# One graph-attention layer on one core: constants behind the first k|v tiles, three empty steps in a tile's tail, a third PSUM tile for projections

## The chip, the cores and the metric

The kernel runs on one core of a Trainium2 chip, in one launch. The metric is the device time of one execution in microseconds (us). Engines are called by the profile's names: PE (matmuls), PEld (loading of its weights), DVE (vector), ACT (scalar, activations), POOL (GpSimd, which also issues the indirect DMAs) and SP (which only issues DMAs).

## The reference

There are 4096 nodes with rows of 512 floats, 8 heads of 64, and an adjacency matrix of 4096 x 4096 with about 0.4% ones besides the diagonal. Everything is float32.

```python
hs = layer_norm(x, ln1_scale, ln1_bias)          # sources
ht = layer_norm(h_target, ln1_scale, ln1_bias)   # targets
q = (ht @ Wq + bq).reshape(T, H, HD) / sqrt(HD)
k = (hs @ Wk + bk).reshape(S, H, HD)
v = (hs @ Wv + bv).reshape(S, H, HD)
logits = where(adj != 0, einsum('thd,shd->hts', q, k), -1e30)
ctx = einsum('hts,shd->thd', softmax(logits), v).reshape(T, D)
ht = ht + (ctx @ Wo + bo)
ht = layer_norm(ht, ln2_scale, ln2_bias)
ff = gelu(ht @ W1) @ W2                           # 512 -> 2048 -> 512
out = plain_norm(x + ht + ff)                     # mean and variance only
```

All node masks are one. If a row had too many edges for the kernel's lists, or another of its assumptions failed, a flag set by `verdict` would send the launch through a second, dense path; with these inputs it does not run.

## The kernel before, in words

The kernel uses the sparsity: per target only the rows of k and v at its edges are fetched. Work comes in tiles of 128 rows.

**Lists.** `edges(i)` reads the 128 adjacency rows of tile i in four quarters of 512 KB (tile "a", two buffers, issued by SP), ACT turns them into signs ("sg", L670), DVE multiplies them with column numbers (L672) and picks the largest in segments (L674), and a few more DVE steps make the list of the row's neighbours. `sort(part)` orders the targets of a part (20 tiles in part A, 12 in part B) by their number of edges; POOL scatters the records into that order by indirect DMAs (L783). A tile of sorted targets then needs only as many slots as its richest row has edges; these numbers are fixed in the tables `CAPS_A` and `CAPS_B` (11 to 40).

**Projections.** `project` walks over groups of two tiles. `norm` loads the rows ("xin", three buffers), DVE takes the statistics, POOL the power -1/2 (L643), and ACT scales. `turn` transposes the group on PE (L834) and ACT copies it out of PSUM into "hT" (L838). For a source tile, `source` makes k and v in two halves of eight matmuls each (L848) into the PSUM tile "pq", ACT copies each half to "row" (L850), and ACT's queue stores the row to the DRAM table kvd (L852). For a target tile, `target` makes q into "pq" (L859); DVE scales it into "row" with the bias bq8 (L862), DVE or POOL fill the other half of "row" with the normed target row times s1b plus bob (L867, L868), and the row goes to the table tqd (L870). "pq" has two buffers, "row" has two. The order is six x groups, then x and h groups by turns, then the remaining h groups.

**Constants.** `late_constants` loads Wq, Wo and four broadcast rows (s1b, b1b, bob, bq8) on SP's queue, zeroes the first row of kvd, scales bq (L619), and makes bv @ Wo on PE into a "pq" tile (L623), which DVE adds to bob (L625, L626). b1b sits in a "row" buffer until L625 has read it. It is called right after the first norm and transposes, ahead of all projections.

**Attention.** A sorted tile is handled in kv segments of up to three slots (210 in all). `issue` lets POOL gather the kv rows of a segment (L895, six kv buffers, four segments ahead) and, at a tile's first segment, the target rows "tq" (three buffers). Per segment DVE multiplies k by q (L1054) and sums per head (L1058), ACT takes the exponential (L1062, L1072), DVE and ACT multiply v (L1019, L1039), and PE adds up the transposed products in "cps" (L1027). When a tile's last segment is through, its tail `finish` runs: sums, 1/sum, copied wide by ACT (L959); transposes of that on PE (L964); copy (L966); multiplication with cps on DVE (L968); product with Wo on PE (L972); sum with the target row on DVE (L975), which is the last reader of "tq"; and for the last tile of a group of two, shift, power, scaling (L987), transposes (L995) and the copy into h2T (L999). `finish` is a generator. At each yield it hands control back, and `attention` calls `advance` twice per segment, each call moving every living tail by one step. The single PSUM buffer "t" serves all tail products.

**Feed-forward.** `feed(g)` waits for h2T of group g, then makes 512 -> 2048 (L1152), gelu on ACT (L1155), and 2048 -> 512 (L1161); `end` adds x, norms and scatters the rows to the output.

**Order.** `_weave` runs several generators in the order of their written costs: a stream that yields a cost is moved on by it, and the stream with the smallest time is served next. In the first weave the streams are `projections`, `prepare` (lists of part A, sort, first prefetch), `fill` and `begin` (first attention steps); in the second one `attention`, the feeds and the lists of part B. What this gives is the order of the program and so the priority of its instructions; the framework places them on the engines' queues, each of which then runs in order.

`projections`, the stream that the change alters, is short:

```python
def projections():
    yield from _some(proj, both * G)
    src.close()
    load_quarter(late.enter_context(tc.tile_pool(name="s2wa", bufs=1)), 0)
    yield from proj
```

`_some(proj, n)` passes on n costs of `proj`, one per k|v or q tile. G is 2, so 2 * G is four tiles.

Of the kernel before, what the change touches and what calls it, by code (L numbers as in the profile page):

```python
# [8 lines left out]
F32 = mybir.dt.float32  # L9
# [8 lines left out]
P = 128  # L18
# [413 lines left out]
def _some(gen, n):  # L432

    while n:
        cost = next(gen, StopIteration)
        if cost is StopIteration:
            return
        n -= cost is not None
        yield cost
# [3 lines left out]
def adj_resnorm_kernel(  # L443
# [34 lines left out]
    N, D = x.shape  # L478
# [4 lines left out]
    G = 2  # L483
# [46 lines left out]
    with tc.tile_pool(name="keep", bufs=1) as keep:  # L530
# [14 lines left out]
        with ExitStack() as late:  # L545
# [61 lines left out]
            def late_constants():  # L607
                zero = wp.tile([P, 2 * D // P], F32, name="zero")
                nc.vector.memset(zero, 0.0)
                nc.sync.dma_start(kvd[0:1, :].rearrange("o (p n) -> (o p) n", p=P), zero)  # L610
                wq = load_w(wp, Wq, "wq", nc.sync)
                nc.sync.dma_start(wo, Wo.rearrange("(c p) n -> p c n", p=P))
                s1b = row_bcast(wp, ln1_scale, "s1b")
                b1b = ip.tile([P, 2 * D], F32, name="row")[:, :D]
                nc.sync.dma_start(b1b, bass.AP(tensor=ln1_bias.tensor, offset=ln1_bias.offset,
                                               ap=[[0, P], [1, D]]))
                bob = row_bcast(wp, bo, "bob")
                bq8 = row_bcast(wp, bq, "bq8")
                nc.vector.tensor_scalar_mul(bq8, bq8, HD ** -0.5)  # L619

                pb = psi.tile([P, D], F32, name="pq", bufs=2)
                for kc in range(KC):
                    nc.tensor.matmul(pb, bvc[:, kc:kc + 1].to_broadcast([P, P]), wo[:, kc, :],  # L623
                                     start=kc == 0, stop=kc == KC - 1)
                nc.vector.tensor_add(bob, bob, b1b)  # L625
                nc.vector.tensor_add(bob, pb, bob)  # L626
                return wq, s1b, bob, bq8
# [166 lines left out]
            def project(order, t=None):  # L794


                state = {}

                def scaled(t, rs, nm):
                    nc.scalar.activation(t, t, AF.Identity, bias=nm, scale=rs)  # L800

                def norm(n, t=None):
                    if n >= len(order):
                        return
                    kind, g = order[n]
                    if t is None:
                        t = ip.tile([P, G, D], F32, name="xin", bufs=3)
                        nc.sync.dma_start(t, rows(x if kind == "x" else h_target, g))
                    if kind == "h" and g * G >= NA:
                        rs, nm = hnorm[0]  # L810
                        for j in range(G):
                            i = g * G + j - NA
                            scaled(t[:, j, :], rs[:, i:i + 1], nm[:, i:i + 1])
                        state[n] = t
                        return
                    mv = ip.tile([P, G, 2], F32, name="mv")
                    for j in range(G):
                        stats(ip, t[:, j, :], mv[:, j, :], "n1")
                    rs, nm = rstd_of(ip, mv, G, "n1")
                    for j in range(G):  # L820
                        scaled(t[:, j, :], rs[:, j:j + 1], nm[:, j:j + 1])
                    state[n] = t

                def turn(n):
                    if n >= len(order):
                        return
                    t = state[n]
                    hT = ip.tile([P, KC, GR], F32, name="hT")
                    for k2 in range(KC // 2):
                        pt = (psi if k2 else ps).tile([P, 2, GR], F32, name="pt" if k2 else "t")  # L830
                        for k in range(2):
                            kc = k2 * 2 + k
                            for j in range(G):
                                nc.tensor.transpose(pt[:, k, j * P:(j + 1) * P],  # L834
                                                    t[:, j, kc * P:(kc + 1) * P], ident)
                        for k in range(2):
                            kc = k2 * 2 + k
                            nc.scalar.activation(hT[:, kc, :], pt[:, k, :], AF.Identity,  # L838
                                                 bias=b1c[:, kc:kc + 1], scale=s1c[:, kc:kc + 1])
                    state[n] = t, hT  # L840

                def source(n, j):
                    g, hT = order[n][1], state[n][1]
                    kvr = ip.tile([P, 2 * D], F32, name="row")
                    for half, w in enumerate((wk, wv)):
                        pkv = psi.tile([P, D], F32, name="pq", bufs=2)
                        for kc in range(KC):
                            nc.tensor.matmul(pkv, hT[:, kc, j * P:(j + 1) * P], w[:, kc, :],  # L848
                                             start=kc == 0, stop=kc == KC - 1)
                        nc.scalar.copy(kvr[:, half * D:(half + 1) * D], pkv)  # L850
                    r0 = 1 + (g * G + j) * P
                    nc.scalar.dma_start(kvd[r0:r0 + P, :], kvr)  # L852
                    return 7.8

                def target(n, j):
                    g, (t, hT) = order[n][1], state[n]
                    pq = psi.tile([P, D], F32, name="pq", bufs=2)
                    for kc in range(KC):
                        nc.tensor.matmul(pq, hT[:, kc, j * P:(j + 1) * P], wq[:, kc, :],  # L859
                                         start=kc == 0, stop=kc == KC - 1)  # L860
                    tq = ip.tile([P, 2 * D], F32, name="row")
                    nc.vector.scalar_tensor_tensor(tq[:, :D], pq, HD ** -0.5, bq8,  # L862
                                                   op0=ALU.mult, op1=ALU.add)
                    part = 1 if g * G >= PARTS[1][0] else 0

                    eng, dma = (nc.vector, nc.sync) if ready else (nc.gpsimd, nc.gpsimd)
                    eng.tensor_mul(tq[:, D:], t[:, j, :], s1b)  # L867
                    eng.tensor_add(tq[:, D:], tq[:, D:], bob)  # L868
                    r0 = (g * G + j - PARTS[part][0]) * P
                    dma.dma_start(tqd[part][r0:r0 + P, :], tq)  # L870
                    return 4.3

                with tc.manual_schedule(engines={mybir.EngineType.DVE}):
                    norm(0, t)
                    turn(0)
                    norm(1)
                yield 0.0
                for n, (kind, _) in enumerate(order):
                    while n + 2 < len(order) and order[n + 2][0] == "h" \
                            and order[n + 2][1] * G >= NA and not hnorm:  # L880
                        yield None
                    for j in range(G):
                        cost = (source if kind == "x" else target)(n, j)
                        if j == 0:
                            turn(n + 1)
                        else:
                            norm(n + 2)
                            del state[n]
                        yield cost
# [53 lines left out]
            def finish(i, p, cps, group, hs, mv):  # L943
# [15 lines left out]
                nc.scalar.copy(rxf.rearrange("p (h d) -> p h d", h=H),  # L959
                               ri.unsqueeze(2).to_broadcast([P, H, HD]))  # L960
                yield
                prx = ps.tile([P, KC, P], F32, name="t")
                for c in range(KC):
                    nc.tensor.transpose(prx[:, c, :], rxf[:, c * P:(c + 1) * P], ident)  # L964
# [1 line left out]
                nc.scalar.copy(ct, prx)  # L966
                yield
                nc.vector.tensor_mul(ct, cps, ct)  # L968
                yield
                pa = ps.tile([P, D], F32, name="t")  # L970
                for c in range(KC):
# [13 lines left out]
                nm = negmean(sp, mv[:, :nh, :], rs, nh, "n2")  # L985
                for j, h in enumerate(hs):
                    nc.scalar.activation(h, h, AF.Identity, bias=nm[:, j:j + 1], scale=rs[:, j:j + 1])  # L987
                yield
                w = len(hs) * P
                h2T = sp.tile([P, KC, 2 * P], F32, name="h2T")  # L990
# [229 lines left out]
            proj = project(order, first_x)  # L1220
            next(proj)
            list_constants()
            wq, s1b, bob, bq8 = late_constants()
            w1, w2 = [], []

            def load_quarter(pool, q):
# [3 lines left out]
                nc.sync.dma_start(w2[q], W2[q * D:(q + 1) * D, :].rearrange("(c p) n -> p c n", p=P))  # L1230

            def projections():
                yield from _some(proj, both * G)
                src.close()
                load_quarter(late.enter_context(tc.tile_pool(name="s2wa", bufs=1)), 0)
                yield from proj
# [86 lines left out]
```

## Time and profile before

| | us |
|---|---|
| median of 5 runs | 1905.1 |
| lowest, highest | 1896.77, 1911.73 |
| profiled execution | 1909.35 |
| its span on the core | 1907.3 |

The profile's page lists the busy time of each engine (matmul ends are modelled, so a busy PE need not be PE at its peak), the span in 40 slices with the granted PE clock and the DMA share, the chain of work that ended last, and the costliest groups of instructions. The largest groups are these.

| line | engine, what | count | busy us |
|---|---|---|---|
| L895 | POOL, issue of the kv gathers | 600 | 701.8 |
| L1161 | PE, 2048 -> 512 | 1024 | 470.8 |
| L1152 | PE, 512 -> 2048 | 2176 | 473.5 |
| L1054 | DVE, k by q | 210 | 351.5 |
| L1058 | DVE, sum per head | 210 | 349.6 |
| L1027 | PE, transposes of v products | 2092 | 268.6 |
| L1019 | DVE, v by weights | 210 | 249.1 |
| L848 | PE, k and v products | 512 | 122.7 + 119.5 |

A wait is idle time of an engine in front of an instruction, put down to what released that instruction. The releaser is inferred, and of several the last is named.

### The profile page before, as it was taken

Reading aid. Unit: us, or ns where it says so; the run is one execution under the profiler, and the core shown is the slowest. Engines: PE = TensorE matmul, PEld = TensorE weight load, DVE = VectorE, ACT = ScalarE, POOL = GpSimd, SP = SyncE. Lnnn points to the kernel's source line nnn. Section 1 sums busy time; section 2 is a strip of 40 time slices with the busy share of each in tenths; the row PEclk is TensorE's granted clock in tenths of the full one; section 3 lists DMA queues with packets and bytes.
Section 4 is the critical chain, followed back from the end, with each engine's and each line's share of the span. In section 5 each row is a group of like instructions: output and inputs, shape, how many; then the busy total and the mean of one; then the engine's idle time right before and its main releaser. Section 6 shows DMA issues by size and latency. Waiting matters only on the chain.

```text
span 1907.3 us, 22630 instructions
## 1 busy us (share of the span) xinstructions
PE 1707.1 (90%) x6974; PEld 1090.4 (57%) x6974; DVE 1506.5 (79%) x2712; ACT 1180.9 (62%) x2943; POOL 938.5 (49%) x847
## 2 busy tenths in 40 slices
PE   6799888687789989988999998988998999999995
PEld 2344343344557666655767675766665766667664
DVE  4778887556989999876787888889999999989601
ACT  4666655444658777565666757676776777766510
POOL 1003322423555445466666665767766777666201
PEclk9999999898999999999999999999998999999998
DMA  8888886689979787666777877889888788777200
GB/s 290 273 273 294 278 260 225 199 315 385 344 272 318 270 319 242 217 223 223 240 256 250 287 265 264 308 276 306 299 280 298 247 300 295 235 266 273 95 1 24
DMA packets 155738, 490.48 MB, mean 257 GB/s; under 512 B 24900, under 2 KB 29592, under 8 KB 155608
## 3 DMA queue, kind: packets, MB, share of 16 engines
q0 software_dynamic: 99040, 355.28, 53.9%
q1 hardware_dynamic: 50864, 114.78, 18.2%
q10 hardware_dynamic: 5704, 18.89, 2.6%
q8 instruction: 57, 0.93, 0.2%
q14 instruction: 73, 0.60, 0.1%
HBM read 441.23 MB, written 47.65 MB: 256 GB/s over the span
## 4 chain that ended last, share of the span: by engine, by line
DVE 25%; DMA 25%; PE 23%; issue 10%; POOL 9%; ACT 6%; SPq 0%; DVEq 0%; POOLq 0%; ACTq 0%
DMA kv<-kvd,rec 12%; DMA a<-in_adj_dram 8%; PE pf L1152 7%; DVE kv L1054 7%; PE po L1161 7%; POOL kv L895 6%; DVE lg L1058 6%; DVE kv L1019 4%; PE t L972 3%; PE cps L1027 3%; ACT sg L670 2%; POOL rec L783 1%; ACT kv L1039 1%; DVE n_st L653 1%; DMA xin<-in_x_dram 1%
## 5 line engine op out<-in xcount | busy, mean ns | idle before, releaser
L895 POOL DMA_INDIRECT kv<-kvd,rec x600 | 701.8, 1170 | 406.2 <-issue 181.2
L1161 PE MATMUL po<-w,gt 128*128 128x512 f32 x1024 | 470.8, 600 | 8.5 <-ACT gt L1155 8.5
L1152 PE MATMUL pf<-h2T,w 128*128 128x256 f32 (+1 forms) x2176 | 473.5, 370 | 1.9 <-ACT h2T L999 1.8
L1054 DVE TENSOR_TENSOR kv<-kv,tq 128x1536 f32<-128x1536 f32 (+2 forms) x210 | 351.5, 1676 | 136.0 <-DMA kv<-kvd,rec 125.8
L1152 PEld LDWEIGHTS pf<-h2T,w 128*128 128x128 f32 x2176 | 388.5, 192 | 67.9 <-issue 20.6
L1039 ACT ACTIVATE kv<-kv,pa 128x64 f32<-128x64 f32 x1512 | 389.4, 335 | 5.0
L1058 DVE TENSOR_REDUCE lg<-kv 128x24 f32<-128x1536 f32 (+2 forms) x210 | 349.6, 1668 | 1.4
L1161 PEld LDWEIGHTS po<-w,gt 128*128 128x128 f32 x1024 | 188.2, 193 | 196.2 <-issue 184.6
L1027 PEld LDWEIGHTS cps<-ident,kv 128*128 128x128 f32 x2092 | 242.6, 143 | 89.7 <-issue 34.3
L1027 PE MATMUL cps<-ident,kv 128*128 128x128 f32 x2092 | 268.6, 276 | 25.3 <-DVE kv L1019 14.8
L1019 DVE TENSOR_TENSOR kv<-kv,p 128x1024 f32<-128x1024 f32 (+1 forms) x210 | 249.1, 1189 | 14.5 <-ACT p L1062 14.5
L670 ACT ACTIVATE sg<-a 128x1024 uint8<-128x1024 int32 x128 | 135.0, 1055 | 145.0 <-DMA a<-in_adj_dram 122.3
L643 POOL TENSOR_TENSOR n_rs<-n_ve,mhalf 128x2 f32<-128x2 f32 (+2 forms) x61 | 48.9, 802 | 336.7 <-DVE n_ve L636 267.3
L972 PE MATMUL t<-wo,rb 128*128 128x512 f32 x256 | 131.5, 661 | 35.2 <-DVE rb L968 35.1
L848 PE MATMUL pq<-wk,hT 128*128 128x512 f32 x256 | 122.7, 624 | 29.9 <-DVE row L862 13.8
L1155 ACT ACT_TABLE_LOAD x114 | 146.3, 1283 | 1.9
L1062 ACT ACTIVATE p<-lg 128x24 f32<-128x24 f32 (+2 forms) x178 | 34.0, 191 | 181.0 <-DVE lg L1058 165.3
L1062 ACT ACT_TABLE_LOAD x91 | 116.8, 1283 | 43.7 <-DVE lg L1058 33.1
L859 PE MATMUL pq<-wq,hT 128*128 128x512 f32 x256 | 123.2, 625 | 16.8 <-DVE row L862 8.7
L848 PE MATMUL pq<-wv,hT 128*128 128x512 f32 x256 | 119.5, 611 | 11.4 <-DVE row L862 9.4
L674 DVE MAX8 cand<-wd 128x8 uint16<-128x103 uint16 (+1 forms) x640 | 127.9, 253 | 1.2
L1155 ACT ACTIVATE gt<-pf 128x512 f32<-128x512 f32 x128 | 76.5, 598 | 80.1 <-PE pf L1152 77.4
(140 smaller groups left out, 1502.6 us busy)
## 6 DMA issues: line engine op xcount, KB each, us to landing
a<-in_adj_dram SPq DMA_DIRECT2D x128, 512.0 KB, 5.1
kvd<-row ACTq DMA_DIRECT2D x32, 512.0 KB, 4.4
tq<-row SPq DMA_DIRECT2D x20, 512.0 KB, 7.4
kv<-kvd,rec POOLq DMA_INDIRECT x600, 5.9
xin<-in_L_gnn_h_target_dram SPq DMA_DIRECT2D x16, 512.0 KB, 7.9
w<-in_L_gnn_W_dram SPq DMA_DIRECT2D x8, 1024.0 KB, 26.8
xin<-in_x_dram SPq DMA_DIRECT2D x15, 512.0 KB, 7.1
tq<-row POOLq DMA_DIRECT2D x12, 512.0 KB, 6.4
```

Source lines behind the costliest of these rows:

```text
L670: nc.scalar.activation(sg, a, AF.Sign, accum_out=dpart[:, i, h:h + 1])
L848: nc.tensor.matmul(pkv, hT[:, kc, j * P:(j + 1) * P], w[:, kc, :], start=kc == 0, stop=kc == KC - 1)
L895: nc.gpsimd.indirect_dma_start(out=dst, out_offset=None, in_=table[:, :], in_offset=bass.IndirectOffsetOnAxis(ap=idx, axis=0))
L972: nc.tensor.matmul(pa, ct[:, c, :], wo[:, c, :], start=c == 0, stop=c == KC - 1)
L1019: nc.vector.tensor_tensor(v4, v4, p[:, j0:j0 + m, :].unsqueeze(3) .to_broadcast([P, m, H, HD]), ALU.mult)
L1027: nc.tensor.matmul(cps[:, c, :], kv[:, j, D + c * P:D + (c + 1) * P], ident, is_transpose=True, start=j0 + j == 0 and c == 0, stop=j0 + n ...
L1039: nc.scalar.mul(v, v, pa[:, hd:hd + 1])
L1054: nc.vector.tensor_tensor(kv[:, :n, :D], kv[:, :n, :D], tq[:, :D].unsqueeze(1).to_broadcast([P, n, D]), ALU.mult)
L1058: nc.vector.tensor_reduce(lg[:, :n, :], kv[:, :n, :D].rearrange("p j (h d) -> p j h d", h=H), AX.X, ALU.add)
L1152: nc.tensor.matmul(pf[:, k, :], w1[(f0 + k) // KC][:, kc, (f0 + k) % KC * P:((f0 + k) % KC + 1) * P], h2T[:, kc, :w], start=kc == 0, stop= ...
L1155: nc.scalar.activation(gt, pf, AF.Gelu_apprx_tanh)
L1161: nc.tensor.matmul(po[j], gt[:, k, j * P:(j + 1) * P], w2[(f0 + k) // KC][:, (f0 + k) % KC, :], start=False, stop=f0 + k == FC - 1, skip_g ...
```

## The change

Three things are changed. `late_constants` is called after the fourth k|v tile, from within the stream of the projections, and what it returns reaches `target` through a list. [...] `finish` yields once more at three places: after 1/sum has been copied wide, before the product with Wo, and before the transposes of the normed rows.

```diff
-                pb = psi.tile([P, D], F32, name="pq", bufs=2)
+                pb = psi.tile([P, D], F32, name="pq", bufs=3)
...
-                        pkv = psi.tile([P, D], F32, name="pq", bufs=2)
+                        pkv = psi.tile([P, D], F32, name="pq", bufs=3)
...
                 def target(n, j):
+                    wq, s1b, bob, bq8 = consts
                     g, (t, hT) = order[n][1], state[n]
-                    pq = psi.tile([P, D], F32, name="pq", bufs=2)
+                    pq = psi.tile([P, D], F32, name="pq", bufs=3)
...
                 nc.scalar.copy(rxf.rearrange("p (h d) -> p h d", h=H),
                                ri.unsqueeze(2).to_broadcast([P, H, HD]))
                 yield
+                yield
                 prx = ps.tile([P, KC, P], F32, name="t")
...
                 nc.vector.tensor_mul(ct, cps, ct)
+                yield
                 yield
                 pa = ps.tile([P, D], F32, name="t")
...
                     nc.scalar.activation(h, h, AF.Identity, bias=nm[:, j:j + 1], scale=rs[:, j:j + 1])
+                yield
                 yield
                 w = len(hs) * P
...
-            wq, s1b, bob, bq8 = late_constants()
+            consts = []
...
             def projections():
-                yield from _some(proj, both * G)
+                yield from _some(proj, 2 * G)
+                consts.extend(late_constants())
+                yield from _some(proj, (both - 2) * G)
                 src.close()
```

## The prediction

> **What bounds the kernel now.** I read the page first, then the busy time in five stretches, then the waits of the stretches that the change touches, then the order of time at two spots.
>
> ```profile
> PE 1707.1 (90%) x6974; PEld 1090.4 (57%) x6974; DVE 1506.5 (79%) x2712; ACT 1180.9 (62%) x2943; POOL 938.5 (49%) x847
> ...
> 0.00:26.00 26.00, 7.98 (x17) 4.18 (x18) 5.82 (x22) 8.32 (x13) 4.78 (x20) 1.00 0.88 305
> 26.00:411.00 385.00, 333.67 (x885) 153.15 (x883) 291.46 (x1113) 224.07 (x410) 81.73 (x85) 0.95 0.78 258
> 411.00:470.00 59.00, 43.72 (x129) 22.73 (x130) 35.62 (x56) 26.75 (x69) 27.11 (x26) 0.88 1.00 396
> 470.00:1800.00 1330.00, 1233.68 (x5563) 850.95 (x5562) 1163.35 (x1500) 911.65 (x2435) 814.85 (x706) 0.97 0.78 269
> ```
>
> The rows of the stretches give, in order, PE, PEld, DVE, ACT and POOL busy, the granted clock, the DMA share and GB/s. Four stretches matter: a start of 26 us in which PE works 8; the projections up to 411, where the last k|v store lands and the first kv gather goes out; a ramp; and attention woven with the feed-forward, where PE is busy 93% and DVE 87%. After 1800 PE has the feed-forward almost alone. So PE is the fullest engine, but in no stretch is it full. The waits of PE, first 26 to 411, then 470 to 1800, name its holes:
>
> ```profile
> PE pq L848 <- DVE row L862: 23.2, 9, 13.2
> PE pq L848 <- ACT row L850: 15.3, 9, 4.1
> PE pq L859 <- ACT row L850: 4.7, 4, 1.9
> ...
> PE t L972 <- DVE rb L968: 35.1, 16, 5.2
> PE t L995 <- ACT h L987: 13.6, 10, 5.0
> PE t L964 <- ACT rb L959: 11.3, 6, 4.0
> ```
>
> Columns: us, times, longest. Above, PE waits for a copy that empties one of the two PSUM tiles "pq". Below, it waits in a tile's tail: at the Wo product (L972), at the transposes of the normed rows (L995) and at the transposes of 1/sum (L964). The chain of waits says how much of this is on the path: up to 415 us it lies 33.4% on DMA "a" (adjacency loads) and 4.0% on the k product; from 470 to 1800 it lies 17.0% on kv gathers, 8.3% on their issue on POOL, and 22.7% on four PE lines (7.7 + 6.6 + 4.5 + 3.9).
>
> **Part 1, the constants.** PE in order of time at the start:
>
> ```profile
> 7.76 0.42 PE L834 MATMUL pt<-ident,xin 128*128 128x128 f32 x1
> 18.97 2.08 PE L623 MATMUL pq<-wo,cols 128*128 128x512 f32 x2 [10.79 <-DMA wo<-in_L_gnn_Wo_dram]
> 20.84 0.85 PE L834 MATMUL t<-ident,xin 128*128 128x128 f32 x3
> 21.48 0.85 PE L834 MATMUL pt<-ident,xin 128*128 128x128 f32 x3
> 22.11 4.13 PE L623 MATMUL pq<-wo,cols 128*128 128x512 f32 x6
> 26.09 1.45 PE L848 MATMUL pq<-wk,hT 128*128 128x512 f32 x3
> ```
>
> The bias product sits in PE's queue and holds the first transposes, so the first k|v matmul comes at 26.09. Without it the transposes run at 7.5 to 9, the four copies to hT (0.5 us each) end near 11, and the v half waits at most for wv (landed at 17.22, taken as no later): tile 1 would end by about 20.8 (17.2 + 3.6) where it now ends at 33.1 (29.5 + 3.6). That is 12 us. SP's seven issues (3.57 to 12.15) leave the front, so the first "a" load goes out some 8 us earlier than 12.25.
>
> What comes back behind four k|v tiles: eight matmuls (8 x 0.45 = 3.6 us, the cadence of the k half), the scaling of bq (0.42) and two adds (0.69 each) on DVE, 8.6 us of SP issues, and 3 MB of loads, 8 us at the 396 GB/s of the ramp. Each stands before others: behind SP's issues the "a" and xin loads; behind DVE's scaling the list steps (L672, L674) and the norm's statistics, for which POOL's power waits; behind PE's bias product the next k|v tile. A load awaited in place costs 10.2 us in the trace (DVE at L625, for bob). b1b also takes one of the two "row" buffers until L625 has read it; a k|v tile then takes about 10.2 us (copy 0.6, second half 3.6, copy 0.6, store landing 5.4) in place of 7.2, 3 us for some two tiles. Against that the DMA share is 0.78 in this stretch, so 8 us of loads are made up in some 40 us, and the first q product is at 146.5, a cover of over 100 us for late constants; were it gone, the 10 us would be paid once more. Of 12 us I keep 8; bounds -3 (two in-place waits eat the gain) and +13.
>
> **Part 2, the third PSUM tile.** Over the whole projections PE waits 51.8 us in 24 pieces for a row copy (38.4 at L848, 13.4 at L859). One more tile lets PE run one more half, 3.6 us, so all but the excess of the longest two (13.2 and 7.3, 13.3 us in all) could go: 38 us. Gaps of 2.6 to 13.2 us here are followed by stretches at half clock, 27 us in all in the trace's clock records (at 93, 213, 240 and 349 us), worth another 13. But this stretch's path is mainly loads of "a", of which only two fit; if PE runs ahead, those loads come last. A fifth of 51 is 10 us; bounds 0 and 25. The feed-forward's PSUM pool takes over these banks at its first use near 506 us; the last q product starts at 469, so 36 us cover that wait.
>
> [...] I go by the waits of this trace, which are for the PSUM copy itself.
>
> **Part 3, the three empty steps.** They stand before the transposes of 1/sum (L964), before the Wo product and before the transposes of h: the three PE waits shown, 62.1 us with L995's 2.1 for h2T. The 210 kv segments take 1366 us (434 to 1800) with two steps each, so a step is 3.25 us; the 36 waits average 1.7 us and only six exceed 3.25, by 7 us together, so nearly all could go. Here the longest seen, and its price:
>
> ```profile
> 708.55 0.94 POOL L895 DMA_INDIRECT kv<-kvd,rec  x1 [8.09 <-PE cps L1027]
> 712.57 0.69 DVE L968 TENSOR_TENSOR rb<-cps,rb 128x512 f32<-128x512 f32 x1
> 713.32 5.06 PE L972 MATMUL t<-wo,rb 128*128 128x512 f32 x6 [5.04 <-DVE rb L968]
> ...
> 708.00:720.00 12.00, 6.96 (x14) 2.95 (x13) 12.00 (x24) 11.16 (x30) 4.44 (x3) 0.72 0.56 168
> ```
>
> PE stands 5.04 us, because the multiplication is late in DVE's queue; then six matmuls take 5.06 us where eight take 3.6: the clock is at half (0.72 in the mean). Eight such gaps in tails (2.9 to 5.2 us) stand at stretches of half clock, 44 us in the clock records, worth 22. So 84 us of PE time hang on these waits at most. A PE microsecond shortens the path only where PE is on it: 22.7% of this stretch. That gives 0.25 x 84 = 21 us; upper bound half of 84, 42, if PE as fullest engine carries the rest along. It can also lose: bounds below zero are the rival on POOL. Next late then are the kv gathers (DVE waits 125.8 us for them now).
>
> [...]
>
> The empty steps cost no instruction. They start the first feed-forward 3 x 3.25 = 10 us later, at 505.8 now, while PE has about a quarter idle (38 of 50 us busy at 450 to 500): 3 us lost. At the end they cost nothing: the last h2T is ready at 1828.2, but the group before keeps PE busy to 1859; those 31 us cover the 10, and without them the full 10 would be paid.
>
> **Sum.** 8 + 10 + 21 - 3 = 36 us. The profiled execution took 1909.35 (span 1907.3); 1909.35 - 36 = 1873.4. The median of five is 4.25 lower, so 1869.
>
> **Rivals.** Slower: the row of 1/sum, the product and h move two steps, 6.5 us, and h is what frees a "tq" buffer (three of them). POOL waits for h 50.0 us in 11 gathers already, and all kv gathers queue behind it in order. If each of the 29 later tq gathers waits 6.5 us more, that is 188 us on POOL; it is spare by 339 (1330 - 815 busy - 176 issue), but gathers and their issue carry 25% of the chain, so 47 us, less about 20 left of the gains: about 1930. It decides once the added wait passes 146 us (36 / 0.25), 23 of 29 gathers. For it: kv gathers are the longest entry of the chain. Against: tq is fetched long before need (the gather at 1264.9 serves a tile that starts after 1340), and its place in POOL's order follows h already (up to a microsecond behind it in about half the tiles), so it should move along.
>
> Tails free, nothing gained: the gathers pace attention, PE's holes move to the kv transposes. Then 8 + 10 - 3 = 15 us: 1890. For it: 125.8 us of DVE waiting for gathers; against: POOL itself waits 83.8 us for PE's transposes, which a tail stall holds up.
>
> The change does little: instructions do not stand as written. PE's bias product is split by transposes above, and the tq gathers run a tile and a half ahead, so the framework orders by its own estimate; it could issue the constants as early as now and put the tails' work where it was. Then perhaps 5 us from PSUM: 1900.
>
> **Numbers.** Forecast 0.57 (own range 1838 to 1890), free tails 0.16 (1880 to 1900), little change 0.07 (1893 to 1910), POOL's wait 0.20 (1912 to 1950). About 0.5% can be told from no change: 1895.6 to 1914.6. Faster: 0.56 + 0.12 + 0.01 = 0.69; same: 0.01 + 0.04 + 0.06 + 0.01 = 0.12; slower 0.19. Leaving out the forecast's fastest end and the upper part of POOL's case, 1838 to 1925 holds some 8 in 10.
>
> **What would show it.** First k|v matmul near 11 to 18 us; the last k|v store landing near 393 instead of 411; waits of L848 and L859 for row copies under 20 us; L972, L995 and L964 under 20 us together; granted clock in attention above 0.97. Wrong: POOL's wait for h over 150 us, DVE's wait for kv gathers well over 126, or PE's wait for wo again in front of the first transposes.

## The result, and the profile after

The changed kernel takes 1914.0 us (median) against 1906.5 us of the kernel before: a ratio of 1.0042, with a 95% interval from 1.003 to 1.0054. The forecast was 1869 us. So the time is inside the range, and within the half per cent that was set as "no change", but it moved to the slower side, and 45 us lie between it and the forecast. The profiled execution took 1912.59 us, with a span of 1910.9 us at a mean granted clock of 0.955 (before: 1909.35, 1907.3 and 0.962). The two spans therefore differ by 3.6 us; the rest of the difference between the medians is scatter of single executions (1897 to 1913 us for the kernel before, 1906 to 1923 after).

New line numbers are one to four higher than before: the k|v products stay at L848, q moves from L859 to L860, the Wo product from L972 to L975, the transposes of h from L995 to L999, those of 1/sum from L964 to L966, the gathers from L895 to L896.

First the page's row of busy times (us and share of the span), then the rows by stretch (busy of PE, PEld, DVE, ACT and POOL, granted clock, DMA share, GB/s), both of the kernel after:

```profile
PE 1711.2 (90%) x6974; PEld 1100.5 (58%) x6974; DVE 1501.8 (79%) x2712; ACT 1174.2 (61%) x2937; POOL 944.5 (49%) x847
```

```profile
0.00:26.00 26.00, 12.79 (x34) 6.57 (x35) 10.57 (x43) 10.96 (x17) 5.47 (x21) 1.00 0.93 334
26.00:411.00 385.00, 335.07 (x872) 153.82 (x871) 286.93 (x1107) 222.69 (x411) 84.02 (x87) 0.94 0.79 260
411.00:470.00 59.00, 45.01 (x141) 23.45 (x140) 35.37 (x45) 26.71 (x67) 25.32 (x24) 0.90 1.00 393
470.00:1800.00 1330.00, 1226.52 (x5544) 855.31 (x5543) 1155.32 (x1489) 902.78 (x2423) 818.99 (x704) 0.97 0.78 268
```

PE is busier in the first 26 us (12.79 in place of 7.98) and by 1.4 us in the projections, and *less* busy in attention (1226.5 in place of 1233.7, with 19 matmuls fewer). The span grew by 3.6 us: PE is busy 4.1 us longer with the same 6974 matmuls, so some of them ran slower, and stands 0.5 us less. What was gained at the start was spent later.

Where it was spent is in PE's waits (us, times, longest), first in the stretch of the projections, then in attention, both after:

```profile
PE pq L848 <- ACT hT L838: 15.9, 8, 3.3
PE pq L848 <- DVE row L863: 9.6, 1, 9.6
PE pq L848 <- ACT row L850: 8.7, 5, 3.8
```

```profile
PE t L975 <- DVE rb L970: 23.5, 10, 6.5
PE t L999 <- ACT h2T L1003: 17.9, 7, 5.2
...
PE t L999 <- ACT h L990: 7.7, 5, 4.7
PE t L999 <- DMA kv<-kvd,rec: 5.8, 1, 5.8
...
PE t L966 <- ACT rb L960: 3.2, 2, 2.8
```

In the projections the waits for a row copy fell from 43.2 us (23.2, 15.3 and 4.7) to 18.3, and in their place PE waits 15.9 us at L848 for the transposed rows hT (2.8 before; 5.6 more at L860): the next tile is not there yet. In attention, the waits at the Wo product and at 1/sum fell from 46.4 to 26.7 us, and those at the transposes of h rose from 15.7 to 31.4. That is 62.1 us before and 58.1 after. The waits moved one link down the same tail. PE's idle time in attention nevertheless grew by 7.2 us. The rest of it lies outside the tails: at the sort of part B (L767, 2.4 to 7.5 us, the latter in one wait), before the feed-forward's first product (1.9 to 5.8) and before its second (8.5 to 10.5).

Summing every gap of PE behind its first instruction from the same traces gives the balance, with the time at half clock from the clock records, which begin at 24.9 us before and at 20.0 us after (each gap and each stretch of half clock is counted where it begins):

| us | before: PE idle | after: PE idle | before: half clock | after: half clock |
|---|---|---|---|---|
| 0 to 26 | 12.1 | 7.0 | none recorded | none recorded |
| 26 to 411 | 52.0 | 49.9 | 41.0 | 51.2 |
| 411 to 470 | 14.6 | 14.0 | 13.7 | 10.2 |
| 470 to 1800 | 96.3 | 103.5 | 75.1 | 92.2 |
| whole span | 200.2 | 199.7 | 145.0 | 170.6 |

The last row also holds the time ahead of PE's first instruction and the end behind 1800 us.

### The profile page after: what moved, and what is told of

Read it like the earlier page. It is cut to its first block, busy times and chain, and to the rows that moved or that the text cites. A ratio compares the mean times of both kernels' runs of the same rounds, so it can differ in the third digit from the quotient of the medians.

```text
span 1910.9 us, 22615 instructions
## 1 busy us (share of the span) xinstructions
PE 1711.2 (90%) x6974; PEld 1100.5 (58%) x6974; DVE 1501.8 (79%) x2712; ACT 1174.2 (61%) x2937; POOL 944.5 (49%) x847
## 3 DMA queue, kind: packets, MB, share of 16 engines
q1 hardware_dynamic: 50864, 114.78, 18.3%
## 4 chain that ended last, share of the span: by engine, by line
PE 33%; DVE 24%; DMA 23%; issue 7%; POOL 7%; ACT 5%; ACTq 0%; DVEq 0%; SPq 0%; POOLq 0%
PE pf L1156 12%; PE po L1165 11%; DMA kv<-kvd,rec 9%; DMA a<-in_adj_dram 9%; DVE kv L1058 6%; PE cps L1031 5%; DVE lg L1062 5%; POOL kv L896 4%; DVE kv L1023 4%; PE t L975 3%; ACT sg L670 2%; DVE n_st L653 1%; DVE cand L674 1%; DMA kvd<-row 1%; POOL rec L783 1%
## 5 line engine op out<-in xcount | busy, mean ns | idle before, releaser
L896 POOL DMA_INDIRECT kv<-kvd,rec x600 | 701.8, 1170 | 394.3 <-issue 195.1
L1165 PE MATMUL po<-w,gt 128*128 128x512 f32 x1024 | 476.9, 604 | 10.5 <-ACT gt L1159 10.5
L1156 PEld LDWEIGHTS pf<-h2T,w 128*128 128x128 f32 x2176 | 393.7, 194 | 73.1 <-issue 22.2
L1031 PEld LDWEIGHTS cps<-ident,kv 128*128 128x128 f32 x2092 | 246.3, 144 | 103.2 <-issue 40.4
L1031 PE MATMUL cps<-ident,kv 128*128 128x128 f32 x2092 | 272.3, 279 | 26.3 <-DVE kv L1023 14.7
L848 PE MATMUL pq<-wk,hT 128*128 128x512 f32 x256 | 123.9, 628 | 24.2 <-ACT hT L838 21.7
L975 PE MATMUL t<-wo,rb 128*128 128x512 f32 x256 | 122.2, 619 | 23.5 <-DVE rb L970 23.5
L848 PE MATMUL pq<-wv,hT 128*128 128x512 f32 x256 | 123.8, 629 | 18.4 <-DVE row L863 9.6
L860 PE MATMUL pq<-wq,hT 128*128 128x512 f32 x256 | 124.2, 630 | 14.7 <-ACT hT L838 14.7
```

The costliest lines, as they stand in the source:

```text
L896: nc.gpsimd.indirect_dma_start(out=dst, out_offset=None, in_=table[:, :], in_offset=bass.IndirectOffsetOnAxis(ap=idx, axis=0))
L975: nc.tensor.matmul(pa, ct[:, c, :], wo[:, c, :], start=c == 0, stop=c == KC - 1)
L1031: nc.tensor.matmul(cps[:, c, :], kv[:, j, D + c * P:D + (c + 1) * P], ident, is_transpose=True, start=j0 + j == 0 and c == 0, stop=j0 + n ...
L1156: nc.tensor.matmul(pf[:, k, :], w1[(f0 + k) // KC][:, kc, (f0 + k) % KC * P:((f0 + k) % KC + 1) * P], h2T[:, kc, :w], start=kc == 0, stop= ...
L1165: nc.tensor.matmul(po[j], gt[:, k, j * P:(j + 1) * P], w2[(f0 + k) // KC][:, (f0 + k) % KC, :], start=False, stop=f0 + k == FC - 1, skip_g ...
```

## The experiments

Each kernel ran beside the kernel before on the same chip. A ratio is its time over that of the kernel before, with the 95% interval in brackets; a figure in us is the ratio less one, times the median of the kernel before there (1903 to 1914 us). The theories carry letters in the expectations: A, the projections are paced by the adjacency loads; B, each part gains what was forecast; C, the third step harms and the other two help; D, any longer tail costs the same, by the later feed-forward; E, attention is paced by gathers, DVE and ACT, and PE's waits are slack; F, PE paces; G, the single tail buffer "t" makes the waits; H, any new order costs; I, longer tails cost as such; J, waits can be cured at their own link; K, a wait cured at one link comes back elsewhere in PE's queue.

**e1_const, the constants alone.**

```diff
+                    wq, s1b, bob, bq8 = consts
...
-            wq, s1b, bob, bq8 = late_constants()
+            consts = []
...
-                yield from _some(proj, both * G)
+                yield from _some(proj, 2 * G)
+                consts.extend(late_constants())
+                yield from _some(proj, (both - 2) * G)
```

> Only the call of the constants is moved. Theory A (the projections are paced by the adjacency loads, and attention by its own loop): the first k|v matmul comes 10 us earlier, some 4 us are left at the last k|v store, and the time is 2 to 6 us shorter than before, or unchanged. Theory B (each part gains what was forecast and only the three together spoil it): 8 us shorter.

Ratio 0.9995 (0.9972 to 1.0018). PE's 12.1 us of idle time before 26 us fall to 7.0, and 3.7 us come back before 411 us (52.0 to 55.7), 6 in attention. One of the waits that come back is 4.2 us for the addition to bob (L626) behind the fourth tile.

**e2_psum, the third PSUM tile alone.**

```diff
-                pb = psi.tile([P, D], F32, name="pq", bufs=2)
+                pb = psi.tile([P, D], F32, name="pq", bufs=3)
...
-                        pkv = psi.tile([P, D], F32, name="pq", bufs=2)
+                        pkv = psi.tile([P, D], F32, name="pq", bufs=3)
...
-                    pq = psi.tile([P, D], F32, name="pq", bufs=2)
+                    pq = psi.tile([P, D], F32, name="pq", bufs=3)
```

> Only the third PSUM tile; the order on every engine's queue is that of before, so the time can only change by waits that end earlier. Theory A: PE's waits for row copies fall from 52 to under 25 us, but the last k|v store lands at most 3 us earlier and the time is 0 to 4 us shorter. Theory B: 10 us shorter.

Ratio 0.999 (0.9965 to 1.0014). Every engine's instructions stand in the same order as before, so only the waits differ. PE's, in the stretch of the projections:

```profile
PE pq L848 <- ACT hT L838: 16.8, 10, 4.3
PE pq L848 <- ACT row L850: 9.8, 7, 2.9
PE pq L848 <- DVE wd L672: 9.6, 1, 9.6
```

The wait for the copy that scales q and adds its bias (L862, 23.2 us) is gone from the list, L850's has fallen by a third; 14 us more are spent on hT at L848 (and 4.4 at L859), and 9.6 in one piece that ends with a list step on DVE (L672). PE's idle time in the stretch is 52.0 us in both kernels. The second longest wait for hT shows what they hang on, first on ACT, then on PE:

```profile
406.49 1.06 ACT L670 ACTIVATE sg<-a 128x1024 uint8<-128x1024 int32 x1 [3.50 <-DMA a<-in_adj_dram]
407.55 1.00 ACT L838 ACTIVATE hT<-t,cols 128x256 f32<-128x256 f32 x2
```

```profile
408.14 1.22 PE L859 MATMUL pq<-wq,hT 128*128 128x512 f32 x1 [3.91 <-ACT hT L838]
```

The copy to hT stands in ACT's queue behind a sign step that waited 3.50 us for an adjacency load. Four of the six waits for hT above 1 us are of this kind, with sign steps that waited 2.4 to 3.5 us. This supports theory A.

**e4_const_psum, both together, and e16_const_psum, the same once more.**

```diff
+                    wq, s1b, bob, bq8 = consts       # as in e1
...
+                pb = psi.tile([P, D], F32, name="pq", bufs=3)    # as in e2, all three
```

> Constants and third PSUM tile without the empty steps. Theory A: 3 to 8 us shorter than before, and so 10 to 15 us shorter than with the steps. Theory B: 18 us shorter. A third reading, that any new order of the attention's instructions costs some us by chance, would show here as a time as long as after's.

> Constants and third PSUM tile again, the kernel of e4_const_psum: both readings expect 1 to 7 us shorter than before; this is for the size of the one gain.

Ratios 0.9979 (0.9954 to 1.0003) and 1.0007 (0.9987 to 1.0027). Both intervals hold 1, and both exclude the forecast 18 us (0.9906). The last k|v rows are sent to the table 5.8 and 8.0 us earlier than before, and nothing of that can be told in the total.

**e3_steps, the three empty steps alone.**

```diff
                 yield
+                yield
                 prx = ps.tile([P, KC, P], F32, name="t")
...
                 nc.vector.tensor_mul(ct, cps, ct)
+                yield
                 yield
...
+                yield
                 yield
                 w = len(hs) * P
```

> Only the three empty steps. Theory A: PE's waits in the tails stay near 60 us in all, because they move to the second pair of h2T transposes, which wait for the one PSUM buffer of the tails, and the time is 5 to 15 us longer. Theory B: waits fall under 30 us and the time is 15 to 20 us shorter.

Ratio 1.0048 (1.0023 to 1.0073), 9 us slower: the whole of the change's loss is here. Before the Wo product and at 1/sum PE's idle time falls from 46.5 to 25.7 us; before the transposes of h it rises from 15.8 to 31.7, and before the feed-forward's first product (pf) from 1.9 to 13.5.

**e5_y1, e6_y2, e7_y3, one step at a time.**

```diff
+                yield      # e5: ahead of the transposes of 1/sum
                 prx = ps.tile([P, KC, P], F32, name="t")
...
+                yield      # e6: ahead of the Wo product
                 pa = ps.tile([P, D], F32, name="t")
...
+                yield      # e7: ahead of the transposes of h
                 w = len(hs) * P
```

> Only the first empty step, before the transposes of 1/sum. Theory C (the third step does the harm, the first two help PE): PE's wait at those transposes falls from 11 to under 4 us, the waits at the h2T transposes stay near 16, and the time is 0 to 5 us shorter than before. Theory D (any tail that is longer starts the feed-forward later, and each step costs alike): 3 us longer.

> Only the second empty step, before the product with Wo. Theory C: PE's wait at that product falls from 35 to about 24 us, the waits at the h2T transposes stay near 16, and the time is 0 to 8 us shorter. Theory D: 3 us longer.

> Only the third empty step, before the transposes for h2T. Theory C: PE's waits at those transposes rise from 16 to about 30 us and the time is 8 to 14 us longer. Theory D: 3 us longer.

Ratios 1.0096 (1.0068 to 1.0124), 1.0013 (0.9991 to 1.0035) and 1.0218 (1.0189 to 1.0248): +18, +2.5 and +42 us, against +9 for all three together. They don't add, none gains, and they don't cost alike, so B, C and D fall. PE's waits in attention say where each went. e6, then e7:

```profile
PE t L996 <- ACT h L988: 45.7, 16, 8.6
...
PE t L973 <- DVE rb L968: 4.9, 4, 1.7
```

```profile
PE t L972 <- DVE rb L968: 33.0, 13, 4.6
PE t L996 <- ACT h2T L1000: 26.3, 10, 4.5
```

The second step does at its own place just what the forecast wanted: the wait at the Wo product falls from 35.1 us to 4.9. But the tail's next product then waits 45.7 us for the scaled rows where it waited 13.6. The third step leaves the Wo product's wait (33.0) and hardly touches the one that it was for, the wait for the scaled rows (13.2 in place of 13.6); it adds 26.3 us at its own place, for ACT's copy out of the single buffer "t" (2.1 before). The first step cures 1/sum (11.3 to 2.5 us of idle time), and idle time at cps doubles, 20.8 to 42.9.

**e8_all_but_y3, the whole change without the third step.**

```diff
+                yield      # ahead of the transposes of 1/sum, as in e5
...
+                yield      # ahead of the Wo product, as in e6
...                         # constants and PSUM as in e4
```

> The whole change without its third empty step. Theory C: 8 to 14 us shorter than after, and so 2 to 8 us shorter than before. Theory D: 3 us shorter than after, and so still longer than before.

Ratio 1.0058 (1.0039 to 1.0078). Taking away the step that costs most when alone gains nothing against the whole change (1.0042).

**e15_step_less, one step fewer.** It takes out the yield that stands between the multiplication and the Wo product.

```diff
                 nc.vector.tensor_mul(ct, cps, ct)
-                yield
                 pa = ps.tile([P, D], F32, name="t")
```

> The kernel before with one step less in a tail: the multiplication by 1/sum and the product with Wo in one step. Theory H: 5 to 25 us longer, although the tail is shorter. Theory I: 0 to 10 us shorter.

Ratio 1.0321 (1.0291 to 1.0351), 61 us slower. PE's wait at the Wo product:

```profile
PE t L971 <- DVE rb L968: 83.3, 22, 9.9
```

Without a step between the two the wait is 83.3 us, with the one of before 35.1, with two (e6) 4.9. So at this link each step lessens the link's own wait when it is changed alone; with the first step beside it (e3, e8, after) 23.5 to 25.6 us are left. Yet the one is worth 61 us of the total and the next nothing. In this trace PE stands 44.0 us longer than before (244.2 in place of 200.2) and the span is 44.1 us longer. "Longer tails cost as such" (I) falls too, and H's 25 us are passed by far.

**e11_dve and e12_pe, less work on one engine.** The first sums the logits over 48 of each head's 64 products; the second makes the Wo product from one chunk of four.

```diff
-  kv[:, :n, :D].rearrange("p j (h d) -> p j h d", h=H),
+  kv[:, :n, :D].rearrange("p j (h d) -> p j h d", h=H)[:, :, :, :HD * 3 // 4],
```

```diff
-                for c in range(KC):
-                    nc.tensor.matmul(pa, ct[:, c, :], wo[:, c, :], start=c == 0, stop=c == KC - 1)
+                nc.tensor.matmul(pa, ct[:, 0, :], wo[:, 0, :], start=True, stop=True)
```

> The kernel before with less work for DVE: the sums per head run over 48 of the 64 products, which leaves out a quarter of each logit; 210 instructions shorter by about 0.42 us, 88 us in all. Theory E: 40 to 80 us shorter. Theory F (PE paces attention): under 20 us shorter.

> The kernel before with less work for PE: the product with Wo takes one of its four chunks, which leaves out three quarters of that product; 192 matmuls of 0.43 us less, 82 us in all. Theory F: 60 to 80 us shorter. Theory E: under 20 us shorter, and PE's idle time from 470 to 1800 rises by 60 us or more.

e11: 1.0096 (1.0062 to 1.0129), 18 us slower, which neither theory had, although DVE is busy 71 us less (1435.7). Its time went into waiting for the same gathers, 125.8 us before, here in DVE's waits:

```profile
DVE kv L1054 <- DMA kv<-kvd,rec: 195.2, 83, 15.4
```

e12: 0.9682 (0.9649 to 0.9714), 61 us faster. Its page:

```profile
PE 1626.1 (88%) x6782; PEld 1060.1 (58%) x6782; DVE 1498.7 (81%) x2712; ACT 1177.4 (64%) x2941; POOL 958.5 (52%) x847
```

81.0 us less on PE shorten the kernel by 61: 0.75 us for each. So PE's time counts, as F has it, and E, on which DVE's loop would pace, falls. Two things were not held fixed: the product is a link of the tail, so the tail gets shorter with it, and the order of PE's queue changes (a line diff moves 276 of its instructions in e11, and 423 in e12 beside the 192 that are left out). And PE's idle time didn't shrink with its work: 216.5 us in place of 200.2.

**e13_lead and e14_lists, another order with the same tails.**

```diff
-            LEAD = 30.0
+            LEAD = 40.0      # e13
...
-                    yield 1.9 * cost
+                    yield 2.0 * cost      # e14
```

> The kernel before with the feed-forward's stream starting 10 later in the weave (LEAD 40 in place of 30), the tails as they were. Theory H (any new order of the instructions gives other waits for PE than the order of before, which happens to fit the chip well; the empty steps cost by that and not as steps): the order of PE's queue hardly changes here, so the time is within 5 us of before. Theory D (a later feed-forward costs): 3 to 10 us longer.

> The kernel before with the lists of part B written as a little dearer in the second weave (2.0 in place of 1.9); no instruction and no tail is changed, only the order. Theory H: 5 to 25 us longer, with more half clock or more idle PE from 470 to 1800. Theory I (the longer tails are what costs): within 3 us of before.

Ratios 1.0013 (0.999 to 1.0035) and 1.0012 (0.9992 to 1.0032), where a line diff of PE's order moves 22 and 733 of 6974 instructions (946 in the changed kernel). An order that differs is no loss by itself; H falls in this general form. Even so the waits shift in e14, where no tail is changed: PE's idle time at 1/sum falls from 11.3 to 3.5 us and that at the transposes of h rises from 15.8 to 28.7, at the same total.

**e9_two_t and e10_two_t_steps, a second buffer "t" for the tails**, without and with the three steps, both with constants and PSUM. In the same edit the exponentials "p" move from PSUM to SBUF.

```diff
-                prx = ps.tile([P, KC, P], F32, name="t")
+                prx = ps.tile([P, KC, P], F32, name="t", bufs=2)
...
-                pa = ps.tile([P, D], F32, name="t")
+                pa = ps.tile([P, D], F32, name="t", bufs=2)
...
-                    pt = ps.tile([P, 2, 2 * P], F32, name="t")
+                    pt = ps.tile([P, 2, 2 * P], F32, name="t", bufs=2)
...
-                                p = ps.tile([P, MAXE, H], F32, name="p")
+                                p = sp.tile([P, MAXE, H], F32, name="p", bufs=1)
...
-            st = wp.tile([5 * KC, P], F32, name="st")
+            st = ip.tile([P, 2 * D], F32, name="row")[:5 * KC, :P]
```

> Constants and third PSUM tile, no empty steps, and two PSUM buffers in place of one for the tails and the first transposes (the exponentials p move to SBUF to free a bank). Theory G (the single buffer makes every tail link wait for the copy of the link before): PE's waits at the h2T transposes fall from 15 to under 5 us and the time is 5 to 15 us shorter than before. Theory E (attention is paced by the loop of gathers, DVE and ACT, and PE's waits are the slack that it leaves, which only change place): PE's idle time from 470 to 1800 stays at 90 to 105 us and the time is within 5 us of before.

> The whole change, its three empty steps too, with two PSUM buffers for the tails and p in SBUF. Theory G: the waits for the copy to h2T (18 us in the changed kernel) go, and the time is 10 to 20 us shorter than the changed kernel, below before. Theory E: PE's idle time stays near 100 us and the time stays 0 to 12 us above before.

Ratios 1.0134 (1.0099 to 1.0168) and 1.0117 (1.0083 to 1.0152). The waits that the buffer was for are gone: the transposes of h wait for no copy any more, and their idle time is 8.8 and 11.0 us, all for the scaled rows (e4 15.3, after 31.6). But in e9 the Wo product waits more, and in e10 the feed-forward's second product stands 33.6 us (10.5 after). PE's wait in e9, attention:

```profile
PE t L973 <- DVE rb L969: 55.4, 19, 5.5
```

These two don't isolate the buffer, though, because with it and the move of "p" comes a price elsewhere, in the group of gathers on POOL (busy, mean ns of one, idle before) of e9:

```profile
L896 POOL DMA_INDIRECT kv<-kvd,rec x600 | 758.5, 1264 | 359.6 <-issue 183.4 <-PE cps L1028 71.7 <-DMA w<-in_L_gnn_W_dram 34.5
```

An issue takes 1264 ns where it took 1170, 57 us more over 600 (1261 in e10). So that the buffer cures its own wait is shown; that it would have been no gain without this price is not.

**e17_two_t_y2 and e18_y2, the second step on top of constants and PSUM**, with and without the second buffer.

```diff
                 yield
+                yield
-                pa = ps.tile([P, D], F32, name="t")
+                pa = ps.tile([P, D], F32, name="t", bufs=2)      # e17 alone, and the rest as in e9
```

> Constants, third PSUM tile, the empty step before the product with Wo, and two PSUM buffers for the tails (p in SBUF). Theory J (each wait can be cured at its own link): the wait at the Wo product falls from the 56 us of e9_two_t to under 20, those at the h2T transposes stay under 15, and the time is 15 to 25 us below e9_two_t, at or under before. Theory K (a wait cured at one link comes back at another place of PE's queue): PE's idle time from 470 to 1800 stays at 100 to 115 us and the time is 5 to 25 us above before.

> Constants, third PSUM tile and the one empty step before the product with Wo. Theory J: 5 us or more below before. Theory K: the wait at the Wo product is under 10 us, the waits at the h2T transposes over 40, and the time is within 6 us of before.

Ratios 1.0093 (1.0057 to 1.013) and 1.0005 (0.9982 to 1.0028). e18 has PE's lowest idle time of all but no gain: 193.7 us in place of 200.2, with PE busy 1717.3 us in place of 1707.1 and 180.5 us at half clock in place of 145.0. Its idle time at the Wo product is 5.5 us and at the transposes of h 50.9, the picture of e6. In e17 it is 22.7 and 33.2, with 20.5 at the second feed-forward product. J, which has each wait cured at its own link, falls. K is what e3, e6, e17 and e18 agree with; e7, whose step cures no wait and adds one, goes beyond it.

No version that does the whole computation beats the kernel before by more than the measurement can tell.

## Why the prediction was wrong

**Part 1 (8 us).** The mechanism was right at the start; the term is too large. After, in order of time at the start, first on ACT, then on PE:

```profile
14.38 0.81 ACT L800 ACTIVATE xin<-xin,n_nm,n_rs 128x512 f32<-128x512 f32 x1 [6.07 <-DVE n_nm L648]
15.10 1.00 ACT L838 ACTIVATE hT<-t,cols 128x256 f32<-128x256 f32 x2
```

```profile
9.06 0.85 PE L834 MATMUL pt<-ident,xin 128*128 128x128 f32 x3
15.70 5.80 PE L848 MATMUL pq<-wk,hT 128*128 128x512 f32 x8 [5.79 <-ACT hT L838]
21.34 3.60 PE L848 MATMUL pq<-wv,hT 128*128 128x512 f32 x8
```

The first k|v matmul comes at 15.70 in place of 26.09, and tile 1 ends at 24.9 where 20.8 was reckoned. Two things were missed. The copies to hT, which were to end near 11, begin at 15.10, since the scaling of the second group's rows stands ahead of them in ACT's queue and ACT stood 6.07 us for it. And the first k half takes 5.80 us where 3.6 was reckoned; the v half right behind it takes 3.60. Of the gain 8.2 us are left after four tiles, 4.7 after the bias product, which now stands behind the fourth tile, and 4.1 at the last k|v store (406.6 in place of 410.7). In e1 the last k|v rows are stored 1.8 us earlier and the total gains nothing. The sum took 8 us for the end of the stage, and the end of the stage for that of the kernel; the runs show neither. It should have asked, for each later tile, what it waits for. Loads of "a" are part of that, as e2's rows show; the chain up to 415 us does not settle how much, since it gives them 33.4% before, 40.4% after and 19.2% in e1.

**Part 2 (10 us).** The waits for row copies fell below 20 us as forecast. But the term was 0, not 10: e2 turns them into other waits, 21.2 us of them for hT, and PE stands 52.0 us as before. The sentence "if PE runs ahead, those loads come last" was right in four of e2's six longer waits for hT, and a fifth was too much. What the forecast went by instead, that the waits "are for the PSUM copy itself", did not hold for ACT's copies: in the kernel before, too, the copy was late for a load: in seven of the eight waits above 1 us for a copy by ACT, a sign step stands ahead of it that waited 1.1 to 4.3 us for "a". One of them, on ACT and then on PE:

```profile
93.42 1.06 ACT L670 ACTIVATE sg<-a 128x1024 uint8<-128x1024 int32 x1 [3.41 <-DMA a<-in_adj_dram]
94.47 1.05 ACT L850 COPY row<-pq 128x512 f32<-128x512 f32 x2
```

```profile
95.09 1.22 PE L848 MATMUL pq<-wk,hT 128*128 128x512 f32 x1 [4.13 <-ACT row L850]
```

The forecast for the last k|v store, 393 us, was missed by far: 406.6 (410.7 before).

**Part 3 (21 us).** This is the step that failed: it cost 9 us in place of bringing 21. Two assumptions stand in it, and the runs separate them. The weight, 0.25 us for a PE microsecond, was if anything too *low*: e12 gives 0.75 for work taken away, and in e15's trace a wait that grew lengthened the span in full (44 us). What was wrong is "so nearly all could go": the three places, forecast below 20 us together, kept 58. They were counted as 36 independent waits, each to be covered by 3.25 us. In fact the tail is a string of short products in PE's queue, between the transposes of the kv segments and the feed-forward, and PE takes them in that order (in e2, where only the waits differ, its instructions stand as before). The reading that fits e3, e6 and e18 is this: a step more ahead of one link puts it later among the other work, so its own wait shrinks; the next links come later against their own inputs and neighbours, and one of them becomes the place at which PE stands. A moved wait, after, on PE and then on ACT:

```profile
1014.04 1.12 PE L999 MATMUL t<-ident,h 128*128 128x128 f32 x4 [5.20 <-ACT h2T L1003]
```

```profile
1011.56 1.28 ACT L1066 ACT_TABLE_LOAD   x1 [2.79 <-DVE lg L1062]
1012.86 0.19 ACT L1066 ACTIVATE p<-lg 128x24 f32<-128x24 f32 x1
1012.99 1.00 ACT L1003 ACTIVATE h2T<-t,cols 128x256 f32<-128x256 f32 x2
```

The second four transposes of h need the buffer "t" that ACT's copy empties. That copy stands in ACT's queue behind an exponential, which waits 2.79 us for DVE's sums of a kv segment: PE stands 5.20 us for a segment of attention that has nothing to do with this tail. In the kernel before, this wait came four times and took 2.1 us in all.

**The clock.** Of the 84 us that the forecast wanted to win a share of, 22 were lost clock behind the tails' gaps, and the granted clock in attention was to pass 0.97. It is 0.97 as before, with more time at half clock (75.1 to 92.2 us). PE's gaps became fewer, 109 to 87, and longer: those over 2.5 us went from 20 to 27. PE was busy at half clock for 121.5 us in place of 101.8, which goes with the 4.1 us by which its busy time grew. That the longer gaps are the cause is not shown: over the kernels the number of gaps above 2.5 us does not fix the time at half clock (e15 has 34 and 160.9 us, e18 has 22 and 180.5). The forecast counted idle time and the clock as falling together; in attention neither fell.

**The rivals.** POOL's wait for h, the slower one, did not happen. POOL's and DVE's waits in attention, after:

```profile
POOL tq L896 <- DVE h L978: 56.1, 11, 9.2
```

```profile
DVE kv L1058 <- DMA kv<-kvd,rec: 132.9, 57, 6.8
```

50.0 us became 56.1, again in 11 gathers, far from the 146 us more at which it would have decided (36 / 0.25 is 144, a slip that changes nothing). The slower result had another cause, for which no case stood: that 1914.0 lies in this case's range (1912 to 1950) is luck. "Tails free, nothing gained" fails since the tails were not freed, and since e12 shows that PE's time counts. "The change does little" (1900, range 1893 to 1910) comes as near by its centre, but not by its reason: the instructions moved, and single steps are worth up to 61 us.

**The 3 us for the later feed-forward** rest on a start 10 us later, which did not come. The first product of 512 -> 2048 starts at 507.4 us before (the 505.8 of the forecast is ACT's copy ahead of it), at 507.7 in e3, at 506.9 in e6, and at 503.3 in the changed kernel. So the runs show nothing for this term.

**What stays open.** The runs show that the three steps bring the loss and that the waits they were meant to end move; why one step more costs 2.5, 18 or 42 us at three places of the same tail, and all three 9, is not derived. The traces show which link waits in each kernel; that its place in the queue comes from the framework's own estimate of when each instruction will be ready, and that this estimate knows nothing of the stalls, is an argument, which no run tests. Whether a second buffer "t" would gain without moving "p" to SBUF was not tried.

## What to carry to other kernels

A wait in an in-order queue is not a sum to be saved (here 62.1 us of PE's waits in the tails became 58.1, and its idle time in attention rose by 7.2): before crediting it, ask which instruction of the same chain comes next and what that one will wait for when it arrives. To learn whether an engine's time counts, take some of its work away (here 81 us of PE gave 61, 71 us of DVE gave nothing) rather than reading a weight off the chain of waits, and look whether the order of the other instructions stayed as it was. When an engine waits for a copy, look at what stands ahead of that copy in its own queue: here four of e2's six waits for hT above 1 us were for copies behind sign steps that waited 2.4 to 3.5 us for a load, and one more PSUM buffer gave a ratio of 0.999. Try the neighbours of a tuned distance in both directions, one at a time: here one step fewer costs 61 us and one more gains nothing, so at this link the distance was already at its bend.

## What the runs showed of the hardware

In these traces half clock came the more often, the longer PE's gap was. Over the traces of before and after, 28 of the 30 gaps above 3.4 us saw a stretch of half clock begin in them or within 4 us of their end (the other two end before the clock records begin), 13 of the 17 between 2.5 and 3.4 us, and 14 of the 37 between 1.5 and 2.5 us. Over the traces of all twenty kernels these are 272 of 309, 118 of 185 and 126 of 365, and 51 of the 677 gaps between 0.5 and 1.5 us; stretches of time picked at random, as long as the gaps of 1.5 to 2.5 us, saw it in 8%. Up to 1800 us the clock records of before and after have 54 stretches at half clock: 31 of 3.4 us, 18 of 6.8, 4 of 10.2 and one of 13.7.

At the start PE was slow too: the first k half of the changed kernel took 5.80 us for eight matmuls and the v half behind it 3.60. The clock records begin only in between, at 20.0 us.

An indirect gather's issue on POOL took 1261 to 1268 ns in the mean in the three kernels with a second buffer "t" and the exponentials in SBUF in place of PSUM (e9, e10, e17), and 1153 to 1191 in the other seventeen. No run here separates the two changes or shows why.
